# Spreading Layer 2's expert gates over the partitions on TensorE instead of through DRAM

## The chip, the cores and the metric

The kernel runs on one of the eight cores of a Trainium2 chip. The metric is the device time of the whole program in microseconds (us), lower is better; the time given is the median of several runs. The kernel before has a median of 1565.0 us over three runs (1563.73, 1565.0, 1570.41).

## The reference, cut to what matters

The program takes x, of four batches x 512 tokens x 128 features in fp32, through four layers of three residual steps each: an FFN, an attention, an FFN. Every FFN step is x + 0.5 * FFN(LN(x)), every attention step x + attn(LN(x)). The change touches the two FFNs of Layer 2, which weigh eight experts by the two largest of eight logits:

```python
def _L2_ffn_ref(x, w_gate, w_in, w_out):
    xt = x.reshape(-1, D)
    logits = (xt @ w_gate.T).astype(jnp.float32)
    top_logits, top_idx = jax.lax.top_k(logits, TOP_K)
    top_gates = jax.nn.softmax(top_logits, axis=-1).astype(x.dtype)
    gates = (jax.nn.one_hot(top_idx, E, dtype=x.dtype) * top_gates[..., None]).sum(axis=1)
    y = jnp.zeros_like(xt)
    for e in range(E):
        h = xt @ w_in[e].T
        y = y + gates[:, e:e + 1] * (h @ w_out[e].T)
    return y.reshape(B, S, D)
...
x = x + 0.5 * _L1_ffn_ref(_layernorm(x, axis=-1), ...)
x = x + 0.5 * _L2_ffn_ref(_layernorm(x, axis=-1), ...)
x = x + _L2_attn_ref(_layernorm(x, axis=-1), ...)
x = x + 0.5 * _L2_ffn_ref(_layernorm(x, axis=-1), ...)
x = x + 0.5 * _L3_ffn_ref(_layernorm(x, axis=-1), ...)
```

Layer 2's attention is a gated linear recurrence over the tokens. Layer 3's FFN sends each token to two of eight experts with limited capacity. There is no nonlinearity between w_in and w_out in Layer 2, so the kernel multiplies the two beforehand into one 128x128 matrix m_e per expert (`prep_l2`, L1197), and y becomes the sum over e of (gate_e * LN(x)) times m_e.

## The kernel before, in words

**Tiling.** A batch is a tile of 128 partitions (tokens) x 4 token groups x 128 features. The batches go in two pairs, [0, 1] and [2, 3]. Matmuls want the features on the partitions, so a normalized batch is transposed on TensorE into one PSUM bank and copied by ScalarE to a 128x512 tile nT: features on the partitions, tokens along the row (`normed_T`, L1022; `transposed`, L176, L180). PSUM is handed out one bank at a time from a ring of eight (`bank`, L56).

**The chain.** L1475 to L1489 hold the stretch that matters. For each pair, the generator `behind` runs Layer 1's second FFN (`l1_ffn`, L1058), Layer 2's first FFN (`l2_ffn`, L1237), its attention (`l2_attn`, L1290), its second FFN and Layer 3's routing (`Mixture.tokens`, L283). `skewed` (L1404) interleaves the two pairs step by step, the second one eight steps behind the first; a step ends at each `yield`. VectorE, ScalarE, TensorE and SyncE's DMA queue are then put in order by a scheduler with a cost model of its own. GpSimd alone is in manual order: its instructions stay as written. After the chain come Layer 3's experts (`experts`, L405), its attention and the rest.

**One Layer 2 FFN of one pair.** (1) The norms: statistics on VectorE (L153, L154), the root on GpSimd (L157 to L162), the scaling on ScalarE (L167). (2) The eight logits of every token on TensorE (`scored`, L1038), the two largest on VectorE (`route`, L205), their sigmoid weights on ScalarE (L1250, L1252). (3) The gates, one tile of 128 tokens x 8 groups x 8 experts (L1254 to L1257). (4) The gates must weigh nT, whose rows run along the tokens, so every one of nT's 128 partitions needs the gate of each token, for each expert. `to_rows` (L1047) transposes the gates of a batch to 8 experts x 512 tokens (L1051), ScalarE copies them out of PSUM (L1053), and SyncE's queue writes them to DRAM (L1055). From there two DMAs per batch (L1265) read four experts each, repeated for all 128 partitions, 1 MB each, into tiles with the tag "spread" (six buffers). (5) VectorE multiplies each expert's 128x512 gates by nT, in place (L1275). (6) TensorE adds up 8 experts x 4 token groups of 128x128 matmuls in one bank per batch (L1278), and VectorE adds half of it to x (L1287). Steps 4 to 6 read:

```python
            rows = to_rows(pool, gates, x, f"{b}_{tag}")
            for u in range(2):
                half = pool.tile([P, NC, S], FP, name=f"gb{u}{b}_{tag}", tag="spread", bufs=6)
                nc.sync.dma_start(
                    half.rearrange("p e s -> p (e s)"),
                    rows[u * NC : (u + 1) * NC, :].rearrange("e s -> (e s)").partition_broadcast(P),
                )
```

**Around it.** Layer 1's FFN uses `to_rows` too and spreads its gates into tiles cb of the same "spread" buffers (L1083, L1085); its matmuls are L1110, L1111 and L1098. Layer 2's attention has its projections at L1298, two activations at L1300 and L1302, a scan over the tokens at L1307 and its output matmuls at L1311. Layer 3's routing makes logits (L322), ranks (L368, L369), and then scatters each token's row to its experts' places in DRAM by indirect DMAs that GpSimd issues (L395), after copies of counts (L392); for pair [2, 3], batch 2 goes three steps ahead of batch 3. Layer 3's experts begin by fetching what was scattered (L415, L417, L426, L436, L442). The attentions elsewhere in the program use 32-row groups of TensorE for their scores (`product`, L586, L587): four matmuls that contract over 32 partitions each, into four banks.

Of the kernel before, what the change touches and what calls it, by code (L numbers as in the profile page):

```python
# [9 lines left out]
FP = mybir.dt.float32  # L10
I32 = mybir.dt.int32
AF = mybir.ActivationFunctionType
ALU = mybir.AluOpType
# [4 lines left out]
P = 128  # L18
# [23 lines left out]
def kernel(ctx: ExitStack, tc: tile.TileContext, a: dict, out: bass.AP):  # L42
# [1004 lines left out]
    def to_rows(pool, gates, i, tag):  # L1047

        pc = bank(f"gT_{tag}")
        for t in range(NT):  # L1050
            nc.tensor.transpose(pc[:E, t * P : (t + 1) * P], gates[:, i * NT + t, :], ident)  # L1051
        gT = pool.tile([E, S], FP, name=f"gT_{tag}", tag="gT")
        nc.scalar.copy(gT, pc[:E, :])  # L1053
        rows = dram.tile([E, S], FP, name=f"rows_{tag}", tag=f"rows_{tag}")
        nc.sync.dma_start(rows, gT)  # L1055
        return rows

    def l1_ffn(pool, i, bs):  # L1058
        tag = f"f1{i}_{bs[0]}"
        G = len(bs) * NT  # L1060
        nTs = yield from normed_T(pool, bs, tag)
        plg = scored(nTs, l1["gate"], tag)
        sc = pool.tile([P, G, E], FP, name=f"sc_{tag}", tag="sc1")
        nc.scalar.activation(sc, plg, AF.Sigmoid)
        yield
        m1, s1 = route(pool, sc, G, "0")
        rest = without(pool, sc, m1, G, -4.0, "0")
# [12 lines left out]
        for x, b in enumerate(bs):  # L1080
            rows = to_rows(pool, comb, x, f"{b}_{tag}")

            cb = pool.tile([P, NC, S], FP, name=f"cb{b}_{tag}", tag="spread", bufs=6)  # L1083
            for u in range(2):
                nc.sync.dma_start(  # L1085
                    cb[u * I1 : (u + 1) * I1],
                    bass.AP(tensor=rows.tensor, offset=rows.offset + u * S, ap=[[0, I1], [2 * S, NC], [1, S]]),
                )
            cbs.append(cb)
        order = [NC] + list(range(NC))  # L1090
        for x, b in enumerate(bs):
# [13 lines left out]

            for k, c in enumerate(order):
                gw = l1["wg"][:, c * P : (c + 1) * P] if c < NC else l1["sg"]
                uw = l1["wu"][:, c * P : (c + 1) * P] if c < NC else l1["su"]
                ps = pair(f"gu{c}_{b}_{tag}")
                nc.tensor.matmul(ps[0], gw, nTs[x], start=True, stop=True)  # L1110
                nc.tensor.matmul(ps[1], uw, nTs[x], start=True, stop=True)  # L1111
                h = pool.tile([P, S], FP, name=f"h{c}_{b}_{tag}", tag="h1", bufs=6)
                nc.scalar.activation(h, ps[0], AF.Silu)
                nc.vector.tensor_tensor(h, h, ps[1], ALU.mult)
                if c < NC:
                    nc.vector.tensor_tensor(h, h, cbs[x][:, c, :], ALU.mult)
# [120 lines left out]
    def l2_ffn(pool, i, bs):  # L1237
        tag = f"f2{i}_{bs[0]}"
        G = len(bs) * NT
        nTs = yield from normed_T(pool, bs, tag)  # L1240
        lg = scored(nTs, l2["gate"], tag)
        yield
        m1, v1 = route(pool, lg, G, "0")
        rest = without(pool, lg, m1, G, -3.0e38, "0")
        m2, v2 = route(pool, rest, G, "1")

        apart = pool.tile([P, G], FP, name=f"apart_{tag}", tag="apart")
        nc.vector.tensor_tensor(apart, v1, v2, ALU.subtract)
        g1 = pool.tile([P, G], FP, name=f"g1_{tag}", tag="g1")
        nc.scalar.activation(g1, apart, AF.Sigmoid)  # L1250
        g2 = pool.tile([P, G], FP, name=f"g2_{tag}", tag="g2")
        nc.scalar.activation(g2, apart, AF.Sigmoid, scale=-1.0)  # L1252
        yield
        gates = pool.tile([P, G, E], FP, name=f"gates_{tag}", tag="comb")  # L1254
        nc.vector.tensor_tensor(m1, m1, bc(g1, [P, G, E]), ALU.mult)
        nc.vector.tensor_tensor(m2, m2, bc(g2, [P, G, E]), ALU.mult)
        nc.vector.tensor_tensor(gates, m1, m2, ALU.add)  # L1257
        yield

        gb = []  # L1260
        for x, b in enumerate(bs):
            rows = to_rows(pool, gates, x, f"{b}_{tag}")
            for u in range(2):
                half = pool.tile([P, NC, S], FP, name=f"gb{u}{b}_{tag}", tag="spread", bufs=6)
                nc.sync.dma_start(  # L1265
                    half.rearrange("p e s -> p (e s)"),
                    rows[u * NC : (u + 1) * NC, :].rearrange("e s -> (e s)").partition_broadcast(P),
                )
                gb += [half[:, e, :] for e in range(NC)]
        yield  # L1270
        for x, b in enumerate(bs):

            po = bank(f"y{b}_{tag}").rearrange("p (t d) -> p t d", d=D)
            for e in range(E):
                nc.vector.tensor_tensor(gb[x * E + e], gb[x * E + e], nTs[x], ALU.mult)  # L1275
            for e in range(E):
                for t in range(NT):
                    nc.tensor.matmul(  # L1278
                        po[:, t, :],
                        gb[x * E + e][:, t * P : (t + 1) * P],  # L1280
                        l2["m"][:, e, :],
                        start=(e == 0 and t == 0),
                        stop=(e == E - 1 and t == NT - 1),
                    )
                if e % 4 == 3:
                    yield
            nc.vector.scalar_tensor_tensor(xs[b], po, 0.5, xs[b], ALU.mult, ALU.add)  # L1287
            yield

    def l2_attn(pool, bs):  # L1290
# [168 lines left out]
    with tc.tile_pool(name="weights12", bufs=1) as mid:  # L1459
        pools["w"] = mid  # L1460
        prep_l1()
        with tc.tile_pool(name="raw2", bufs=1) as pool:
            made = prep_l2(pool)
            next(made)
            next(made)
            f01.experts(l0["w"], made.send)
            whole(made)
        for b in range(NB):
            whole(f01.combine(b))
        with tc.tile_pool(name="ffn10", bufs=2) as pool:  # L1470
            whole(skewed([l1_ffn(pool, 0, bs) for bs in pairs], 5))

        l1_attn(lambda pool: prep_l3_ffn(xs[0]))

        def behind(pool, bs):  # L1475
            yield from l1_ffn(pool, 1, bs)
            yield from l2_ffn(pool, 0, bs)
            yield from l2_attn(pool, bs)
            yield from l2_ffn(pool, 1, bs)
            if bs[0] == 0:  # L1480
                yield from f30.tokens(bs, l3["gate"], "scalar", pool, later=4)
            else:
                yield from skewed([f30.tokens([b], l3["gate"], "scalar", pool) for b in bs], 3)

        with tc.tile_pool(name="chain", bufs=2) as pool:
            decay = pool.tile([P, S], FP, name="decay", tag="decay", bufs=1)
            nc.gpsimd.memset(decay, 0.9)
            with tc.manual_schedule(engines={mybir.EngineType.Pool}):
                whole(skewed([behind(pool, bs) for bs in pairs], 8))  # L1489
        pools["w"] = wpool  # L1490
# [44 lines left out]
```

## Time and profile before

| | |
|---|---|
| median of three runs | 1565.0 us |
| the profiled execution, its own time | 1562.17 us |
| its span, first to last instruction | 1560.5 us |
| TensorE matmuls (PE) | 1264.9 us busy, 81% |
| TensorE weight loads (PEld) | 821.3 us busy, 53% |
| VectorE (DVE) | 864.1 us busy, 55% |
| ScalarE (ACT) | 712.9 us busy, 46% |
| GpSimd (POOL) | 655.7 us busy, 42% |
| DMA traffic | 123.12 MB |
| mean granted TensorE clock | 0.893 of full |

The profile is of one execution, which the hardware recorded; its lines are sorted by source line and engine. A line such as "L1278 PE MATMUL y_f<-m,gb_f 128*128 128x128 f32" names source line, engine, operation, output and inputs, tile of the array and shape. An fp32 matmul leaves two records, so a count of 8 is four matmuls. In a timeline, the first column is the start in us from the beginning of the span and the second how long the row's instructions took together; the text in square brackets is how long the engine sat idle before and what ended that. SPq is SyncE's DMA queue. The chain from Layer 1's second FFN to Layer 3's routing lies between about 777 and 1051 us of the span. The four Layer 2 FFNs have their gates done at 845.7 (pair 0, first), 879.5 (pair 1, first), 936.9 (pair 0, second) and 975.4 us (pair 1, second). The tags of these four in the order named are f20_0, f20_2, f21_0 and f21_2.

### The profile page before, as it was taken

What the parts mean: (1) busy time and instruction counts of PE and PEld (TensorE: products, weight loads), DVE (VectorE), ACT (ScalarE), POOL (GpSimd) and SP (SyncE); (2) the same over time, 40 slices, a digit from 0 to 9 for tenths busy, and PEclk for the clock granted to TensorE, in tenths of its full rate; (3) what the DMA queues carried; (4) which work ended last, traced back from release to release, by engine and by line L of the source; (5) the groups of instructions that cost most, each with busy time, mean ns of one, the idle gap of its engine ahead of it and who ended that gap; (6) DMA issues with size and microseconds to landing.
All of it is one profiled execution on the core that took longest, in us unless ns stands there. A gap on an engine that the chain in (4) does not pass through costs nothing. (4 is left out here: it accounts for less than half of the span.)

```text
span 1560.5 us, 28691 instructions
## 1 busy us (share of the span) xinstructions
PE 1264.9 (81%) x10523; PEld 821.3 (53%) x10523; DVE 864.1 (55%) x2947; ACT 712.9 (46%) x1487; POOL 655.7 (42%) x789
## 2 busy tenths in 40 slices
PE   4777998995969688989988676718779999998394
PEld 3455676773756455766756655616533343333273
DVE  5335676773325365766556455515367787774343
ACT  1234876871443165768643322203325655564041
POOL 3455767872520176777501111273632214212253
PEclk9997999996979888999999778758979999999597
DMA  7420240002515474442033302214204000000223
GB/s 231 129 57 8 77 164 12 9 13 64 148 35 109 126 226 123 136 123 69 2 78 116 135 0 109 114 50 114 64 21 171 14 3 13 12 5 15 75 79 105
DMA packets 103092, 123.12 MB, mean 79 GB/s; under 512 B 9404, under 2 KB 74152, under 8 KB 100904
## 3 DMA queue, kind: packets, MB, share of 16 engines
q1 hardware_dynamic: 96296, 108.07, 23.2%
q0 software_dynamic: 6656, 13.22, 2.6%
q8 instruction: 84, 1.38, 0.4%
q14 instruction: 56, 0.46, 0.1%
HBM read 79.27 MB, written 41.98 MB: 78 GB/s over the span
## 5 line engine op out<-in xcount | busy, mean ns | idle before, releaser
L605 POOL TENSOR_SCALAR sc_a<-sc_a,top_a 128x128 f32<-128x128 f32 (+3 forms) x256 | 275.4, 1091 | 112.1 <-DVE top_a L604 72.2
L587 PE MATMUL s_a<-k_a,q_a 32*128 32x512 f32 (+3 forms) x1536 | 267.1, 549 | 17.9 <-DMA k_a<-fac_a 14.2
L692 ACT ACTIVATE w_a<-t_a 128x512 f32<-128x512 f32 x256 | 140.4, 595 | 119.7 <-PE t_a L587 94.8
L628 PE MATMUL t_a<-ident,sc_a 128*128 128x128 f32 x1280 | 172.3, 282 | 6.0 <-DVE top_a L608 5.6
L489 POOL DMA_INDIRECT res_f<-y_f,back_f x112 | 109.7, 980 | 141.8 <-ACT y_f L488 101.3
L587 PE MATMUL t_a<-ql_a,k_a 32*128 32x512 f32 x512 | 168.8, 643 | 0.5 <-DVE low_a__12599 L672 0.2
L628 PEld LDWEIGHTS t_a<-ident,sc_a 128*128 128x128 f32 x1280 | 145.1, 144 | 36.8 <-issue 13.8
L617 ACT ACTIVATE sc_a<-sc_a,top_a 128x128 f32<-128x128 f32 (+3 forms) x256 | 135.0, 577 | 23.8 <-DVE top_a L608 23.6
L587 PEld LDWEIGHTS s_a<-k_a,q_a 32*128 32x128 f32 x1536 | 93.7, 188 | 88.9 <-issue 43.1
L637 ACT ACTIVATE w_a<-t_a 128x256 f32<-128x256 f32 (+2 forms) x192 | 94.2, 526 | 64.2 <-PE t_a L628 63.7
L395 POOL DMA_INDIRECT disp_f<-n_f,to_f x96 | 94.3, 983 | 66.8 <-issue 58.8
L501 PE MATMUL o_f<-w_l,h_f 128*128 128x128 f32 (+1 forms) x896 | 113.0, 279 | 3.8 <-DVE o_f L483 3.3
L501 PEld LDWEIGHTS o_f<-w_l,h_f 128*128 128x128 f32 (+1 forms) x896 | 103.0, 184 | 14.7 <-DVE o_f L483 6.0
L466 PE MATMUL h_f<-dT_f,w_l 128*128 128x320 f32 (+1 forms) x256 | 107.8, 559 | 2.8 <-ACT dT_f L444 2.8
L157 POOL TENSOR_SCALAR rs_f<-mv_f 128x4 f32<-128x4 f32 (+1 forms) x23 | 6.5, 281 | 233.4 <-DVE mv_f L154 232.7
L650 PE MATMUL acc_a<-w_a,vpad 128*32 128x128 f32 x2560 | 98.4, 280 | 0.6 <-DVE top_a L604 0.6
L639 ACT COPY w_a<-t_a 128x256 f32<-128x256 f32 (+2 forms) x192 | 93.7, 528 | 6.7 <-PE t_a L628 6.5
L672 DVE TENSOR_REDUCE low_a__12599<-s_a 128x1 f32<-128x512 f32 x128 | 82.1, 685 | 26.3 <-PE t_a L587 18.5
L608 DVE CUSTOM_DVE_ANT_0 sc_a<-s_a,future 128x128 f32<-128x128 f32 (+3 forms) x128 | 62.3, 487 | 57.2 <-PE s_a L587 44.2
L672 DVE TENSOR_REDUCE low_a__12597<-s_a 128x1 f32<-128x512 f32 x128 | 81.3, 683 | 20.5 <-PE t_a L587 15.1
L608 DVE CUSTOM_DVE_ANT_0 sc_a<-s_a,table 128x128 f32<-128x128 f32 (+3 forms) x128 | 62.4, 487 | 53.0 <-PE s_a L587 52.5
L488 ACT ACTIVATE y_f<-o_f,d_f 128x128 f32<-128x128 f32 (+1 forms) x112 | 38.8, 394 | 105.9 <-DVE o_f L483 102.3
(337 smaller groups left out, 2260.8 us busy)
## 6 DMA issues: line engine op xcount, KB each, us to landing
gb_f<-rows_f SPq DMA_DIRECT2D x16, 1024.0 KB
fac_a<-fac_a_sb SPq DMA_DIRECT2D x36, 256.0 KB
disp_f<-zeros_f SPq DMA_DIRECT2D x4, 2080.0 KB
d_f<-disp_f SPq DMA_DIRECT2D x32, 260.0 KB
w_l<-in_L_ffn_w_dram SPq DMA_DIRECT2D x16, 512.0 KB
cb_f<-rows_f SPq DMA_DIRECT2D x16, 512.0 KB
q_a<-fac_a SPq DMA_DIRECT2D x32, 256.0 KB
k_a<-fac_a SPq DMA_DIRECT2D x32, 256.0 KB
```

Source lines behind the costliest of these rows:

```text
L395: nc.gpsimd.indirect_dma_start(out=self.to[c][i0 + t][:, :], out_offset=bass.IndirectOffsetOnAxis(ap=to[:, c, t : t + 1], axis=0), in_=ns[ ...
L466: nc.tensor.matmul(ps[u][:, :cap], w1[:, e, (c + u) * P : (c + u + 1) * P], dT, start=True, stop=True)
L489: nc.gpsimd.indirect_dma_start(out=self.back[e * per + s][:, :], out_offset=bass.IndirectOffsetOnAxis(ap=back[:m, s : s + 1], axis=0), in_ ...
L501: nc.tensor.matmul(po[:m, s, :], h[:, c, s * P : s * P + m], w2[:, e, c, :], start=(c == 0), stop=(c == NC - 1),)
L587: nc.tensor.matmul(ps[:, n0:n1], q[r : r + SLOT, i * P : (i + 1) * P], k[r : r + SLOT, n0:n1], start=True, stop=True)
L605: nc.gpsimd.tensor_scalar(sc, sc, top, None, ALU.subtract)
L608: nc.vector.tensor_tensor_reduce(sc, banks[r][:, :n], more, -1.0, HUGE, ALU.add, ALU.min, top)
L617: nc.scalar.activation(sc, sc, AF.Exp, bias=top, scale=-1.0)
L628: nc.tensor.transpose(ps[:, x * n + j * P : x * n + (j + 1) * P], st["sc", u, i, r0 + x][:, j * P : (j + 1) * P], ident,)
L650: nc.tensor.matmul(st["acc", u][r * SLOT : (r + 1) * SLOT, i * P : (i + 1) * P], vpads[b % 2][:, j, g * 4 + r, :], st["w", u, i, r][:, j * ...
L672: nc.vector.tensor_reduce(st["low", u][:, i, c : c + 1], ps, AX.X, ALU.max, negate=True)
L692: nc.scalar.activation(w, ps, AF.Exp)
```

## The change

The gates no longer go through DRAM. They are written into a tile of 128 tokens x 8 groups x 128 columns that lives as long as the chain, one per pair, set to zero once on GpSimd. Expert e = 2r + u has column 32r + u, so the transpose of a group, now 128x128, puts it on partition 32r + u: each of the four 32-row groups r of TensorE holds two experts. One ScalarE copy of 128x512 per batch brings this into SBUF (gT). Two constant tiles `row[u]` of 128x128 hold ones on the partitions p with p % 32 = u, zeros elsewhere. Four matmuls that contract over 32 partitions, one in each row group, of `row[u]` and gT then put the gates of four experts on all 128 partitions, each in a PSUM bank of its own; VectorE multiplies each bank by nT into a tile of the new tag "gb" (eight buffers). A batch takes two such rounds, u = 0 and 1. The sixteen y matmuls of a round are issued one round later (`down`), after the next round's four.

The DMAs of Layer 2's rows and broadcasts disappear; Layer 1's FFN keeps its own, and "spread" has four buffers in place of six. An FFN of Layer 2 has one `yield` less. Line numbers after: zeroed tiles L1506, `row` L1511 to L1514, gates L1261, transposes L1267, copy L1269, y matmuls L1281, residual L1290, row-group matmuls L1298, multiplies L1301.

```diff
@@ l1_ffn
-            cb = pool.tile([P, NC, S], FP, name=f"cb{b}_{tag}", tag="spread", bufs=6)
+            cb = pool.tile([P, NC, S], FP, name=f"cb{b}_{tag}", tag="spread", bufs=4)
@@ l2_ffn
-        gates = pool.tile([P, G, E], FP, name=f"gates_{tag}", tag="comb")
+
+        gates = l2["gates", bs[0]]
+        parted = gates.rearrange("p g (r c) -> p g r c", c=SLOT)[:, :, :, : E // 4]
         nc.vector.tensor_tensor(m1, m1, bc(g1, [P, G, E]), ALU.mult)
         nc.vector.tensor_tensor(m2, m2, bc(g2, [P, G, E]), ALU.mult)
-        nc.vector.tensor_tensor(gates, m1, m2, ALU.add)
+        for u in range(E // 4):
+            one, two = (m.rearrange("p g (r u) -> p g r u", r=4)[:, :, :, u] for m in (m1, m2))
+            nc.vector.tensor_tensor(parted[:, :, :, u], one, two, ALU.add)
         yield
-
-        gb = []
+        gTs = []
         for x, b in enumerate(bs):
-            rows = to_rows(pool, gates, x, f"{b}_{tag}")
-            for u in range(2):
-                half = pool.tile([P, NC, S], FP, name=f"gb{u}{b}_{tag}", tag="spread", bufs=6)
-                nc.sync.dma_start(
-                    half.rearrange("p e s -> p (e s)"),
-                    rows[u * NC : (u + 1) * NC, :].rearrange("e s -> (e s)").partition_broadcast(P),
-                )
-                gb += [half[:, e, :] for e in range(NC)]
+            pc = bank(f"gT{b}_{tag}")
+            for t in range(NT):
+                nc.tensor.transpose(pc[:, t * P : (t + 1) * P], gates[:, x * NT + t, :], ident)
+            gT = pool.tile([P, S], FP, name=f"gT{b}_{tag}", tag="gT2", bufs=2)
+            nc.scalar.copy(gT, pc)
+            gTs.append(gT)
         yield
...
+        def down(x, u):
+
+            if u == 0:
+                pos[x] = bank(f"y{bs[x]}_{tag}").rearrange("p (t d) -> p t d", d=D)
+            for r in range(4):
                 for t in range(NT):
                     nc.tensor.matmul(
-                        po[:, t, :],
-                        gb[x * E + e][:, t * P : (t + 1) * P],
-                        l2["m"][:, e, :],
...
+                        pos[x][:, t, :],
+                        gb[x, u, r][:, t * P : (t + 1) * P],
+                        l2["m"][:, r * (E // 4) + u, :],
...
+        rounds = [(x, u) for x in range(len(bs)) for u in range(E // 4)]
+        for x, u in rounds + [(None, None)]:
+            if x is not None:
+                banks = [bank(f"gate{u}{r}_{x}_{tag}") for r in range(4)]
+                for r in range(4):
+                    rows = slice(r * SLOT, (r + 1) * SLOT)
+                    nc.tensor.matmul(banks[r], l2["row"][u][rows, :], gTs[x][rows, :], start=True, stop=True)
+                for r in range(4):
+                    gb[x, u, r] = pool.tile([P, S], FP, name=f"gb{u}{r}_{x}_{tag}", tag="gb", bufs=8)
+                    nc.vector.tensor_tensor(gb[x, u, r], banks[r], nTs[x], ALU.mult)
+            if (x, u) != rounds[0]:
+                down(*rounds[rounds.index((x, u)) - 1 if x is not None else -1])
             yield
@@ the chain's setup
+            for bs in pairs:
+                l2["gates", bs[0]] = pool.tile([P, 2 * NT, P], FP, name=f"gates{bs[0]}", tag=f"gates{bs[0]}", bufs=1)
+                nc.gpsimd.memset(l2["gates", bs[0]], 0.0)
+
+            l2["row"] = []
+            for u in range(E // 4):
+                flag = pool.tile([P, 1], FP, name=f"flag{u}", tag=f"flag{u}", bufs=1)
+                nc.vector.tensor_reduce(flag, ident.rearrange("p (r c) -> p r c", c=SLOT)[:, :, u], AX.X, ALU.add)
+                row = pool.tile([P, P], FP, name=f"row{u}", tag=f"row{u}", bufs=1)
+                nc.vector.tensor_copy(row, flag.to_broadcast([P, P]))
+                l2["row"].append(row)
```

More of the change, by code (lines that the diff above doesn't have):

```diff
@@ L1270, in l2_ffn @@
-        yield
[L1271 to L1276, printed above, removed]
+            pc = bank(f"gT{b}_{tag}")
+            for t in range(NT):
+                nc.tensor.transpose(pc[:, t * P : (t + 1) * P], gates[:, x * NT + t, :], ident)
+            gT = pool.tile([P, S], FP, name=f"gT{b}_{tag}", tag="gT2", bufs=2)
@@ L1277, in l2_ffn @@
+            nc.scalar.copy(gT, pc)
+            gTs.append(gT)
+        yield
+        pos, gb = {}, {}
+        def down(x, u):
+            if u == 0:
+                pos[x] = bank(f"y{bs[x]}_{tag}").rearrange("p (t d) -> p t d", d=D)
+            for r in range(4):
                 for t in range(NT):
                     nc.tensor.matmul(
-                        po[:, t, :],
-                        gb[x * E + e][:, t * P : (t + 1) * P],
-                        l2["m"][:, e, :],
-                        start=(e == 0 and t == 0),
@@ L1283, in l2_ffn @@
-                        stop=(e == E - 1 and t == NT - 1),
-                    )
-                if e % 4 == 3:
-                    yield
-            nc.vector.scalar_tensor_tensor(xs[b], po, 0.5, xs[b], ALU.mult, ALU.add)
+                        pos[x][:, t, :],
+                        gb[x, u, r][:, t * P : (t + 1) * P],
+                        l2["m"][:, r * (E // 4) + u, :],
+                        start=(u == 0 and r == 0 and t == 0),
+                        stop=(u == E // 4 - 1 and r == 3 and t == NT - 1),
+                    )
@@ new lines, in down @@
+            if u == E // 4 - 1:
+                b = bs[x]
+                nc.vector.scalar_tensor_tensor(xs[b], pos[x], 0.5, xs[b], ALU.mult, ALU.add)
+        rounds = [(x, u) for x in range(len(bs)) for u in range(E // 4)]
[10 more added lines that the diff above has]
+                down(*rounds[rounds.index((x, u)) - 1 if x is not None else -1])
```

## The prediction

> **What bounds the kernel now.** I read the page's busy shares first: TensorE (PE) is busy 81% of the span, VectorE (DVE) 55%, so PE decides on average. The change is confined to the chain of Layer 1's last FFN, Layer 2 and Layer 3's routing, so I went on to the list of waits for 835 to 1060 us, where this chain lies. Its columns are total us, number of waits, and the longest.
>
> ```profile
> DVE n_f L415 <- DMA disp_f<-n_f,to_f: 27.9, 1, 27.9
> ...
> DVE gb_f L1275 <- DMA gb_f<-rows_f: 21.6, 4, 8.3
> PE y_f L1278 <- DVE gb_f L1275: 20.7, 4, 7.1
> ...
> PE T_f L180 <- ACT n_f L167: 3.0, 1, 3.0
> ```
>
> There are four Layer 2 FFN instances (two FFNs, two pairs of batches), and each waits once: DVE for the broadcast gates, PE for DVE. So 20.7 us of PE idle time stand in front of exactly the step that the change replaces. Next I read the timeline of the last instance, to see the wait's parts.
>
> ```profile
> 975.13 0.23 DVE L1257 TENSOR_TENSOR gates_f<-mask,mask 128x64 f32<-128x64 f32 x1
> 975.41 1.87 PE L1051 MATMUL gT_f<-ident,gates_f 128*8 128x128 f32 x8 [6.26 <-DVE gates_f L1257]
> ...
> 977.01 1.03 ACT L1053 COPY gT_f<-gT_f 8x512 f32<-8x512 f32 x2
> 977.60 0.76 SPq L1055 DMA_DIRECT2D rows_f<-gT_f  x2
> ...
> 979.12 1.82 SPq L1265 DMA_DIRECT2D gb_f<-rows_f  x4
> ...
> 983.65 2.50 DVE L1275 TENSOR_TENSOR gb_f<-gb_f,nT_f 128x512 f32<-128x512 f32 x4 [8.29 <-DMA gb_f<-rows_f]
> ...
> 984.44 1.83 PE L1278 MATMUL y_f<-m,gb_f 128*128 128x128 f32 x7 [5.46 <-DVE gb_f L1275]
> ```
>
> From gates to first multiply are 8.3 us (975.36 to 983.65), of which 6 lie between the write of the rows (977.60) and the landing of the first broadcast. The other three legs take 8.3, 8.3 and 8.7 us. The stretches beside it show a second loss; the number after the busy times is the granted PE clock.
>
> ```profile
> 982.00:984.00 2.00, 0.00 (x0) 0.00 (x0) 0.35 (x1) 0.00 (x0) 0.00 (x0) 0.69 1.00 410
> 984.00:986.00 2.00, 1.56 (x7) 1.59 (x8) 2.00 (x4) 0.00 (x0) 0.00 (x0) 0.50 1.01 422
> 986.00:988.00 2.00, 2.00 (x12) 2.00 (x11) 2.00 (x5) 0.00 (x0) 0.00 (x0) 0.50 1.01 426
> ...
> 990.00:992.00 2.00, 2.00 (x21) 2.00 (x20) 0.00 (x0) 0.00 (x0) 0.00 (x0) 1.00 0.10 41
> ```
>
> After the idle time PE runs at half clock for some 5 us. The same 16 matmuls (32 records) of L1278 take 3.74 us at full clock (at 896.51) but 6.41, 6.48 and about 6.25 us right after the second, third and fourth wait: 2.5 to 2.7 us lost three times. The first wait is short (2.7 us) and the clock stays up.
>
> Does a gain in this chain reach the end? The chain that ended last names almost only PE work after 1125 us, so I followed what hangs on the chain's last result, x of batch 3 (L1287, 1005.06 us):
>
> ```profile
> 1007.35 0.22 POOL L157 TENSOR_SCALAR rs_f<-mv_f 128x4 f32<-128x4 f32 x1 [3.61 <-DVE mv_f L154]
> ...
> 1009.94 1.13 POOL L395 DMA_INDIRECT disp_f<-n_f,to_f  x1 [0.15 <-POOL n_f L392]
> ```
>
> GpSimd (POOL) keeps the written order; it waits for DVE's statistics of batch 3 at 1007.35, then issues 32 scatters at 1.265 us each, and the 27.9-us wait at L415 above ends only after the last, at 1052.68. PE's 34.5-us wait for the fetched rows (L442) follows. So an earlier x of batch 3 moves the scatters and all behind them one for one.
>
> **What the Trainium skill says.** "TensorE: Matmul & The Clock Gate", Part 3 (packing small matmuls): four K=32, N=512 tiles in four row groups give 3.07 times the rate. The trace has this form in the attention's scores:
>
> ```profile
> 750.91 1.14 PE L587 MATMUL s_a<-k_a,q_a 32*128 32x512 f32 x8
> 751.99 0.33 PE L628 MATMUL t_a<-ident,sc_a 128*128 128x128 f32 x1
> ```
>
> Eight records are four matmuls: 1.08 us until the next instruction starts, against 4 x 0.86 = 3.44 for ordinary 128x512 matmuls (two of L1298 take 1.71): a factor of 3.2, in agreement. In 500 to 800 us, 16 such groups are 19.7 us busy, 1.23 each. "TensorEngine Tiling (Array Packing)", Key Properties and Gotcha 1: changing the tiling mode drains TensorE, and each row tile needs its own PSUM bank. The 1.08 us stand between instructions of other modes, so a drain is in them; the banks are a risk below. "TensorE: Matmul & The Clock Gate", Part 1: idle time of about 3.4 us halves the clock and as much work restores it. The trace agrees roughly: idle from 979.0, halved at about 983.6; full again after some 5 us of work. "DMA: Bandwidth & Descriptors", Anatomy of one DMA, gives about 2 us fixed per DMA, mostly completion; its fit is for GpSimd's queue. Two chained DMAs on SP measured 6 us here, so the order of size agrees.
>
> **The change part by part.**
> *Removed.* Eight row writes and sixteen 1-MB broadcasts: 24 issues on SP and 16 MB. SP has nothing due behind them in the chain, and no one else waits for the DMA rings there, so this is worth only its wait. The new leg: one more DVE add (0.2), four transposes (half of 1.87), one ACT copy (0.6, the 128x512 form takes 0.59), the first group (1.1, or 2.2 at half clock), one multiply (0.7): about 3.5 to 4.6 us until the first y matmul, against 9.1 now (975.36 to 984.44). In that time PE has the eight transposes, the second group, and the other pair's work. I leave 0.7 us of idle time for each of legs two to four (copy and multiply, less one group), none for the first, where Layer 1's matmuls cover most of the wait already. With the shorter gap I expect the clock to be up when y begins.
> *Added on PE.* Four groups per instance, 16 in all. Price 1.08 us, ends 1.23 (busy) and, overlap failing, 3.44. None are hidden: PE is the leading engine in y. 4 x 1.08 = 4.3 per instance. The transposes are 128 instead of 8 columns wide; those of L180, of that form, take the same 1.04 us for eight at full clock: no cost.
> *Changed on DVE.* The 64 multiplies read PSUM in place of SBUF: 0.687 us (L1114) against 0.685. Four are 2.7 us per round, PE needs 3.74 + 1.08 = 4.8: hidden under PE, at no cost while PE is the slower one.
> *ACT.* Copies of 128x512 in place of 8x512: 0.59 against 0.57; nothing.
> *Setup.* Two memsets on POOL (about 0.9 us each, half of the 1.8 of 128x2048) between the memset of 0.9 and the first norm, and four small DVE operations. POOL then waited 1.35 us for DVE at 779.21, so some 0.5 us stay; but Layer 1's first normalized tile is ready at 785 and its transposes start only at 797.18: hidden. Without that cover it would cost 0.5.
> *Moved.* By the instruction orders, outside the Layer 2 FFNs nothing changes places. At the third leg, the transposes that today wait 3.0 us instead of 1.04 for ACT (960.86) come to stand inside y: 2.0 us regained. DVE has Layer 3's routing of batch 2 between the last instance's multiplies; a routing step that waits would hold them.
>
> Sum, leg by leg (idle gone + clock + moved, against groups and idle left): first −2.7 + 4.3 = +1.6. Second −5.4 − 2.6 + 4.3 + 0.7 = −3.0. Third −7.1 − 2.7 − 2.0 + 4.3 + 0.7 = −6.8. Fourth −5.5 − 2.5 + 4.3 + 0.7 = −3.0. Together −11.2. A group takes four of eight banks at once, and its last bank comes free only by a multiply of the group before it or by the other pair's ACT and DVE work; the trace shows no such wait, so its bounds are 0 and about 1.1 us per instance (a group's slot lost); I take 0.5, in all +2.0. Below zero is excluded, since no bank is freed sooner. That gives −9.2. The profiled execution took 1562.2 us (span 1560.5 and 1.7 around it): 1553.0. The runs' median is 1565.0, 2.8 above: 1555.8, say 1556.
>
> **The rivals.** *B, the wait is replaced.* The clock stays halved at the start of y (the three 2.5s are not regained, +7.8) since the new steps are short with gaps: −9.2 + 7.8 = −1.4, 1564. For it: in the fourth leg PE does transposes from 975.4 to 979 and still starts y at half clock. Against: 980 to 983 showed full clock, it fell during the wait. *C, slower: the groups do not overlap.* 16 groups at p us cost 16p against 17.3 in my sum: −9.2 − 17.3 + 16p. It decides from p = 1.66 upward. In pairs (p about 2.2) it is +8.7, 1574; one after the other (3.44) +28.5, 1594. Against it: the same form runs at 1.08 and 1.23. For it: this group's four outputs must find four banks free at once, which could space them out. *D, nothing reaches the end*: the scatter train starts when it does now, because something else than batch 3's x holds POOL: 1565. Against it: POOL waited 3.61 us just there.
>
> **How the numbers follow.** As forecast (A) 0.64, 1554 to 1561 (no bank waits: −11.2, 1554; 1.1 each: −6.8, 1558; 1.23 a group: +2.4 more); B 0.22; D 0.06; C 0.08. I count 0.5% (7.8 us) as what a measurement of this kernel can tell from no change: faster means under 1557.2. Of A, 0.52 lies there and 0.12 above; with B and D, no change has 0.40; C is slower, 0.08. The range from 1550 (no bank waits, none of the 2.1 us of idle time left, and the first leg's 1.6 covered: −14.9) to 1566 holds A, B and D and leaves out C and a little of the rest.
>
> **What would show it.** L1275's and L1278's waits for DMA and DVE gone, under 3 us left in front of y; 16 groups of eight 32x512 records at 1.1 to 1.2 us each; y's first 32 records at 3.7, not 6.4 us; the step to x of batch 3 and the first scatter both 9 us earlier (1000.8 from 1009.9), and L415's wait ending as much earlier. Wrong, if y starts at half clock, if DVE idles inside y for routing steps, if groups last over 1.66 us, or if later stages lengthen by what the chain gives.

## The result, and the profile after

The changed kernel takes 1558.1 us in the median of six runs (1553.6 to 1560.3), against 1566.5 us for six runs of the kernel before: a ratio of 0.9945, with a 95% interval of 0.9933 to 0.9957, or 8.4 us less. The forecast was 1556 against 1565, 9 less. The profiled execution took 1557.3 us, with a span of 1555.6 (before: 1562.2 and 1560.5).

The list of waits for the same stretch, 835 to 1060 us, of the changed kernel:

```profile
DVE n_f L415 <- DMA disp_f<-n_f,to_f: 28.1, 1, 28.1
...
DVE x L1290 <- PE y_f L1281: 17.8, 7, 4.9
...
DVE gb_f L1301 <- PE gate_f L1298: 2.8, 4, 1.2
```

The waits for the broadcast (21.6 us on DVE, 20.7 on PE) are gone, and a line of PE waiting for the multiplies no longer appears. DVE waits for PE instead, at the end of y: PE leads, as forecast. The wait behind the scatters is as long as before (28.1 against 27.9): nothing there was shortened, it was moved.

The fourth leg on the timeline (start, duration):

```profile
972.06 0.32 DVE L1261 TENSOR_TENSOR gates<-mask,mask 128x32 f32<-128x32 f32 x2
...
975.20 1.08 ACT L1269 COPY gT_f<-gT_f 128x512 f32<-128x512 f32 x2
...
976.41 2.00 PE L1298 MATMUL gate_f<-gT_f,row 32*128 32x512 f32 x16
...
977.57 1.29 DVE L1301 TENSOR_TENSOR gb_f<-gate_f,nT_f 128x512 f32<-128x512 f32 x2 [0.57 <-PE gate_f L1298]
...
978.34 0.94 PE L1281 MATMUL y_f<-m,gb_f 128*128 128x128 f32 x6
```

From the gates to the first y matmul are still 6.0 us (972.38 to 978.34), not the forecast's 3.5 to 4.6: ScalarE copies the gates only after Layer 3's two normalized tiles. But PE sits idle in none of it. It does transposes, Layer 3's logits and two of the four groups (a group: the four row-group matmuls of one round), and the clock is up when y begins. The stretches show it (PE's busy time first, the granted clock after the five busy times):

```profile
974.00:976.00 2.00, 2.00 (x18) 2.00 (x18) 0.00 (x0) 1.28 (x3) 0.00 (x0) 0.90 0.00 0
976.00:978.00 2.00, 2.00 (x21) 1.29 (x20) 0.88 (x3) 1.82 (x3) 0.00 (x0) 1.00 0.04 8
978.00:980.00 2.00, 2.00 (x18) 1.66 (x15) 2.00 (x6) 0.00 (x0) 0.00 (x0) 1.00 0.00 0
```

y's first 16 matmuls (32 records) take 3.84 us here. In the second and the third leg they take as long; before, they took 6.25 to 6.48 us in these three legs:

```profile
892.69 3.84 PE L1281 MATMUL y_f<-m,gb_f 128*128 128x128 f32 x32
...
946.12 3.84 PE L1281 MATMUL y_f<-m,gb_f 128*128 128x128 f32 x32
```

The groups' price, by form, in 840 to 1010 us (busy us, mean ns of one record, idle before):

```profile
L1281 PE MATMUL y_f<-m,gb_f 128*128 128x128 f32 x512 | 60.7, 277 | 0.0
...
L1298 PE MATMUL gate_f<-gT_f,row 32*128 32x512 f32 x128 | 18.9, 634 | 0.4 <-ACT gT_f L1269 0.4
```

Sixteen groups are 18.9 us busy, 1.18 each; from the start of a group until the next instruction starts are 1.07 (852.18 to 853.25). y has no idle time before it and is 60.7 us busy in place of 67.5. GpSimd's first step for batch 3 and the first scatter:

```profile
1001.05 0.22 POOL L157 TENSOR_SCALAR rs_f<-mv_f 128x4 f32<-128x4 f32 x1 [3.52 <-DVE mv_f L154]
...
1003.65 1.13 POOL L395 DMA_INDIRECT disp_f<-n_f,to_f  x1 [0.15 <-POOL n_f L392]
```

Before, they stood at 1007.35 and 1009.94. The chain itself must be read from its own start, because the time ahead of it differs from one execution to the next. The next table, from the timelines, gives the us from the start of GpSimd's memset of 0.9 to the arrival of each leg's logits (DVE's first maximum) and to the first scatter.

| kernel | leg 1 | leg 2 | leg 3 | leg 4 | first scatter |
|---|---|---|---|---|---|
| before | 62.4 | 94.6 | 152.3 | 191.9 | 232.6 |
| after | 62.4 | 96.7 | 152.4 | 186.5 | 224.3 |
| first FFN alone | 64.0 | 98.2 | 152.8 | 191.9 | 232.6 |
| second FFN alone | 62.4 | 94.7 | 152.5 | 186.6 | 224.5 |
| broadcasts unread | 62.5 | 96.7 | 152.5 | 186.7 | 224.6 |
| groups twice | 62.4 | 100.1 | 159.0 | 195.7 | 237.2 |
| ordinary matmuls | 62.6 | 105.5 | 170.4 | 211.9 | 261.2 |
| before, clock kept (4 each) | 62.6 | 94.9 | 149.8 | 188.9 | 230.2 |
| before, clock kept (5, 7, 6) | 62.4 | 94.5 | 149.5 | 188.2 | 227.6 |
| after, clock kept | 62.4 | 96.7 | 152.4 | 186.6 | 223.7 |
| hybrid | 62.5 | 94.6 | 146.3 | 175.0 | 220.4 |
| hybrid, clock kept | 62.4 | 94.5 | 146.3 | 175.0 | 214.0 |

The chain is 8.3 us shorter. The pair of profiled spans differs by 4.9 only, since the chain began 2.0 us later (779.33 against 777.34) and 1.4 more lay behind the first scatter (551.95 against 550.56). Both vary as much between other traces (starts from 775.5 to 783.2; in the kernel before with the clock kept by four matmuls 550.3 behind the scatter, with each group twice 553.0), so neither is put down to the change, and the six runs a side agree with the chain.

Each row of the table is one execution, and TensorE's clock can shift it. Up to the first leg's logits TensorE has the same order of work in all twelve kernels, and yet they come 1.6 us later in the kernel with the first FFN alone. Differences of 1 to 2 us between rows need the runs, or a cause on the timeline, beside them.

### The profile page after: what moved, and what is told of

Read it like the earlier page. It is cut to its first block, busy times and chain, and to the rows that moved or that the text cites. A ratio compares the mean times of both kernels' runs of the same rounds, so it can differ in the third digit from the quotient of the medians.

```text
span 1555.6 us, 28883 instructions
## 1 busy us (share of the span) xinstructions
PE 1279.9 (82%) x10651; PEld 823.0 (53%) x10651; DVE 866.6 (56%) x2955; ACT 713.2 (46%) x1487; POOL 657.2 (42%) x791
## 5 line engine op out<-in xcount | busy, mean ns | idle before, releaser
L587 PE MATMUL s_a<-k_a,q_a 32*128 32x512 f32 (+3 forms) x1536 | 266.5, 548 | 17.1 <-POOL k_a L1183 13.8
L692 ACT ACTIVATE w_a<-t_a 128x512 f32<-128x512 f32 x256 | 140.4, 595 | 119.6 <-PE t_a L587 94.9
L395 POOL DMA_INDIRECT disp_f<-n_f,to_f x96 | 94.6, 985 | 66.7 <-issue 58.8
L608 DVE CUSTOM_DVE_ANT_0 sc_a<-s_a,table 128x128 f32<-128x128 f32 (+3 forms) x128 | 62.4, 488 | 52.9 <-PE s_a L587 52.4
```

The costliest lines, as they stand in the source:

```text
L395: nc.gpsimd.indirect_dma_start(out=self.to[c][i0 + t][:, :], out_offset=bass.IndirectOffsetOnAxis(ap=to[:, c, t : t + 1], axis=0), in_=ns[ ...
L587: nc.tensor.matmul(ps[:, n0:n1], q[r : r + SLOT, i * P : (i + 1) * P], k[r : r + SLOT, n0:n1], start=True, stop=True)
L608: nc.vector.tensor_tensor_reduce(sc, banks[r][:, :n], more, -1.0, HUGE, ALU.add, ALU.min, top)
L692: nc.scalar.activation(w, ps, AF.Exp)
```

## The experiments

Four of the kernels below (second FFN alone, broadcasts unread, clock kept with 5, 7, 6, and clock kept in the changed kernel) ran on a chip on which the kernel before took 1585.6 us, so the ratios are what is compared, not the times.

**Each group twice.** The four row-group matmuls of a round are issued twice:

```diff
                 for r in range(4):
                     rows = slice(r * SLOT, (r + 1) * SLOT)
                     nc.tensor.matmul(banks[r], l2["row"][u][rows, :], gTs[x][rows, :], start=True, stop=True)
+                for r in range(4):
+                    rows = slice(r * SLOT, (r + 1) * SLOT)
+                    nc.tensor.matmul(banks[r], l2["row"][u][rows, :], gTs[x][rows, :], start=True, stop=True)
```

> Every row-group matmul of the gates is issued twice into the same bank, the second one overwriting the first with the same values: sixteen groups more. Theory (PE leads in y and in the legs, the chain's end moves the program's end one for one): 16 x 1.07 = 17.1 us more than the changed kernel, less some 1.5 us where PE waits anyway in the third leg, so +15 to +17, which is +7 to +9 against the kernel before. Rival (PE has slack in these stretches or the scatters start when they do anyway): under +5 against the changed kernel, still faster than before.

Measured: 1568.7 us, ratio to before 1.0015 (1.0007 to 1.0023); in the chain 12.9 us more than the changed kernel. The direction is the theory's, the size is less. The timeline says why:

```profile
848.34 1.14 PE L1298 MATMUL gate_f<-gT_f,row 32*128 32x512 f32 x8
849.30 1.04 PE L1301 MATMUL gate_f<-gT_f,row 32*128 32x512 f32 x8
850.27 0.38 PE L1098 MATMUL o_f<-wd1T,h_f 128*128 128x128 f32 x1
```

Two groups take 1.93 us from first start to the next instruction, one takes 1.07: the second adds 0.86. That is the time of one ordinary 128x512 matmul. The other 0.21 us are spent once for each time that PE goes over to row groups and back. 16 x 0.86 = 13.8; the missing 0.9 fits the idle time of the third leg, 1.5 us in the changed kernel and 0.6 here. PE has hardly any slack in the chain. By the two ratios the program takes 11.0 us more than the changed kernel, which within their intervals is what the chain lost; against the kernel before it is 2.3 us (1.1 to 3.6), of 4.6 in the chain.

**Ordinary matmuls in place of row groups.** The case of rival C of the prediction, built. The rows of `row` are not built:

```diff
-                    rows = slice(r * SLOT, (r + 1) * SLOT)
-                    nc.tensor.matmul(banks[r], l2["row"][u][rows, :], gTs[x][rows, :], start=True, stop=True)
+                    nc.tensor.matmul(banks[r], ident[:, r * SLOT + u : r * SLOT + u + 1].to_broadcast([P, P]), gTs[x], start=True, stop=True)
```

> The gates are spread by ordinary matmuls over all 128 rows, one 128x512 per expert, with a column of the identity as weights, instead of four 32-row matmuls at once. Theory (the row groups overlap; that is what makes the change pay): 16 x (3.44 - 1.07) = +38 us against the changed kernel, less 1 to 3 for drains and idle time that go: +35 to +38, slower than before by 26 to 30. Rival (the groups are no faster than ordinary matmuls, or PE has slack): under +10 against the changed kernel.

Measured: 1590.3 us, ratio 1.0161 (1.0145 to 1.0176), slower than before; the chain is 36.9 us longer than in the changed kernel (in the slowest of the five executions, 1595.8 us). On the timeline a round's four now take 3.44 us:

```profile
852.31 3.60 PE L1297 MATMUL gate_f<-gT_f,ident 128*128 128x512 f32 x8
855.75 1.95 PE L1098 MATMUL o_f<-wd1T,h_f 128*128 128x128 f32 x16
```

So the change pays only because a group's four matmuls run at once: without that, the same way around DRAM loses 25 us.

This kernel also shows what going over to row groups costs the work beside a group. The 16 y matmuls between two rounds, first in the changed kernel, then here:

```profile
861.14 3.84 PE L1281 MATMUL y_f<-m,gb_f 128*128 128x128 f32 x32
```

```profile
860.97 3.73 PE L1281 MATMUL y_f<-m,gb_f 128*128 128x128 f32 x32
```

From their start to that of the next round are 3.77 us between groups (to 864.91) and 3.57 here (to 864.54). Of the 0.2 more about half falls behind a group and half ahead of the next, since in the changed kernel the y that follows a group but does not precede one takes 3.67 (865.98 to 869.65). So a group that stands alone costs about 1.27 us and not 1.07; 0.4 of it are for the change of tiling.

**The broadcasts kept, unread.**

```diff
             gTs.append(gT)
+            rows = dram.tile([E, S], FP, name=f"rows_{b}_{tag}", tag=f"rows_{b}_{tag}")
+            nc.sync.dma_start(rows, gT[:E, :])
+            for u in range(2):
+                half = pool.tile([P, NC, S], FP, name=f"gone{u}{b}_{tag}", tag="spread", bufs=4)
+                nc.sync.dma_start(
+                    half.rearrange("p e s -> p (e s)"),
+                    rows[u * NC : (u + 1) * NC, :].rearrange("e s -> (e s)").partition_broadcast(P),
+                )
```

> The changed kernel, with the eight row writes and the sixteen 1-MB broadcasts still issued after ScalarE's copies, into spread tiles that nobody reads. Theory (only the wait for them cost time, not the issues on SyncE's queue nor the 16 MB): within 1.5 us of the changed kernel. Rival (part of the gain came from the traffic that is gone, or from SyncE's shorter list): 3 us or more slower than the changed kernel.

Measured: ratio 0.9934 (0.9917 to 0.9951), and the table's line is the changed kernel's to 0.3 us. The 24 issues and 16 MB have no cost of their own that was measured; what the change removed was the wait, with what the wait did to the clock.

**The kernel before, with TensorE kept at work in the wait.**

```diff
                 gb += [half[:, e, :] for e in range(NC)]
+        if (i, bs[0]) != (0, 0):
+            idle = bank(f"idle_{tag}")
+            for r in range(4):
+                nc.tensor.matmul(idle, ident, nTs[-1], start=True, stop=True)
         yield
```

> The kernel before, with four 128x512 matmuls into an unread bank after the transposes of the gates of the second, third and fourth leg, so that PE works while the broadcast is under way; nothing else is changed and the wait stays. Theory (2.5 to 2.7 us of each of these three waits' cost is the halved clock after it): 5 to 8 us faster than before, y's first 32 records in 3.7 to 4.5 us instead of 6.4. Rival (the halved clock only follows the wait and would cost nothing, or the filler delays what it stands before): within 1 us of before, or slower.

Measured: 1562.9 us, ratio 0.9987 (0.9979 to 0.9996), 2.4 us less in the chain: less than half of the 5 to 8 that were expected. Four matmuls filled only the second leg's wait. In the third, 3.6 us of idle time were left and the first 32 records of y still took 6.42 us, in the fourth 2.1 and 5.44. So the number was raised to 5, 7 and 6:

```diff
-            for r in range(4):
+            for r in range({(0, 2): 5, (1, 0): 7, (1, 2): 6}[i, bs[0]]):
```

> The kernel before with matmuls into an unread bank in the second, third and fourth wait, as in clock4, but five, seven and six of them in place of four each, since in clock4 idle time of 3.6 and 2.1 us was left in the third and fourth wait and y still ran at half clock there (6.42 and 5.44 us for the first 32 records, 3.81 in the second leg). Theory: with the idle time under 1.5 us the clock is up in all three, 6 to 8 us faster than before. Rival (the clock is no cost by itself): no faster than clock4, 2.7 us under before.

Measured: ratio 0.9954 (0.9936 to 0.9971), 7.3 us (4.6 to 10.1), and 5.0 us less in the chain. y after the second, third (two lines) and fourth wait:

```profile
894.68 3.81 PE L1282 MATMUL y_f<-m,gb_f 128*128 128x128 f32 x32 [1.03 <-DVE gb_f L1279]
...
949.53 3.84 PE L1282 MATMUL y_f<-m,gb_f 128*128 128x128 f32 x32 [1.45 <-DVE gb_f L1279]
...
964.28 5.37 PE L1282 MATMUL y_f<-m,gb_f 128*128 128x128 f32 x32
...
986.69 3.81 PE L1282 MATMUL y_f<-m,gb_f 128*128 128x128 f32 x32
```

All three now start at full clock, with the wait for the broadcast still there (22.3 us on VectorE): 5 us or somewhat more of the wait's cost was the clock alone. In the third leg part was lost again: behind a later wait for ScalarE's tiles, which stood there before too, the next 32 records now take 5.37 us in place of 3.74.

**One FFN alone.** The changed `l2_ffn` for the second FFN and the former one for the first, and then the other way round ("spread" has four buffers in both). The former one stands beside it as `l2_ffn_dram`; of the edit only the call is given, in short:

```diff
-            yield from l2_ffn(pool, 0, bs)
+            yield from l2_ffn_dram(pool, 0, bs)
```

> Only Layer 2's second FFN (legs three and four) takes the row groups; its first FFN (legs one and two) goes through DRAM as before. Theory (legs add up as their steps were sized): the first two legs together gained 1.4 us in the changed kernel's profile against before (+1.9 and -3.3), legs three and four 8.3, so this kernel lies about 8 us under before, within 2 us of the changed kernel. Rival (the order that the scheduler chooses for the whole chain decides more than the legs): off from that by over 3 us, with the other order to be seen on TensorE.

> Only Layer 2's first FFN (legs one and two) takes the row groups, the second one goes through DRAM as before: the other half of the kernel named second. The forecast's steps gave +1.6 and -3.0 for these two legs, -1.4 in all. Theory after the runs so far (in the changed kernel the logits of the third leg come at the same distance from the chain's begin as before, 152.4 against 152.3 us, since the 3.3 us won in the second leg go to steps at half clock before the third, and the second FFN alone had the whole gain): within 1 us of before. Rival (each FFN brings half of the gain): about 4 us faster than before.

Measured: the second FFN alone 0.9937 (0.9920 to 0.9955), the first alone 0.9991 (0.9978 to 1.0005). Legs three and four alone bring the whole gain. What the first FFN's change brings can't be told from zero, nor from the forecast's 1.4 us: the interval goes from 3.4 us less to 0.8 more. Its row in the table has a shift that isn't the edit's. Layer 1's matmuls just ahead of the first leg's logits ran in part at half clock here, in the changed kernel in 1.02 us each:

```profile
839.41 1.91 PE L1110 MATMUL gu_f<-nT_f,sg1T 128*128 128x512 f32 x2
841.12 1.50 PE L1111 MATMUL gu_f<-nT_f,su1T 128*128 128x512 f32 x2
```

From the first leg's logits to the third's this kernel is 1.1 us shorter than before (88.8 against 89.9), the changed kernel is not (90.0).

**Only the first leg through DRAM.** The call, again in short:

```diff
-            yield from l2_ffn(pool, 0, bs)
+            yield from (l2_ffn_dram if bs[0] == 0 else l2_ffn)(pool, 0, bs)
```

> The changed kernel, but the first leg (first FFN of batches 0 and 1) takes the way through DRAM as before; the other three use the row groups. The spread tiles have four buffers. Theory (legs add up, and in the first leg Layer 1's matmuls cover most of the broadcast, so the four groups cost 1.6 to 1.9 us there): 1.5 to 2 us faster than the changed kernel, about 10 faster than before. Rival (legs don't add up, or the broadcast into fewer buffers starts later): the same as the changed kernel or up to 3 us slower.

Measured: 1552.5 us, ratio 0.9915 (0.9902 to 0.9928), better than both kernels, by more than the 1.5 to 2 us under the changed kernel that were expected (4.7 by the ratios, 3.9 in the chain). The first leg gives its 2.1 us. The rest is more than the sum of the legs: by the logits of leg four the hybrid is 11.5 us ahead of the changed kernel, and then loses 7.6 of it. The scheduler put TensorE in another order. In the hybrid, the second leg's gates are transposed before the attention's tiles and not among them, and ScalarE copies them 103.8 us after the chain's start in place of 108.5. That this order explains the whole difference is read from the two timelines; it was not tried by itself.

**The hybrid, with TensorE kept at work in the fourth leg.** What the hybrid loses in its last leg is on its timeline:

```profile
963.21 2.01 PE L180 MATMUL T_f<-ident,n_f 128*128 128x128 f32 x5 [4.18 <-ACT n_f L167]
965.15 2.07 PE L1298 MATMUL gate_f<-gT_f,row 32*128 32x512 f32 x2
967.15 0.90 PE L180 MATMUL T_f<-ident,n_f 128*128 128x128 f32 x3
967.98 2.08 PE L1298 MATMUL gate_f<-gT_f,row 32*128 32x512 f32 x6
970.00 3.58 PE L322 MATMUL lg_f<-gate,nT_f 128*128 128x8 f32 x16
973.51 2.09 PE L1298 MATMUL gate_f<-gT_f,row 32*128 32x512 f32 x8
975.53 4.98 PE L1281 MATMUL y_f<-m,gb_f 128*128 128x128 f32 x32
```

After 4.2 us of idle time everything runs at half clock for some 15 us, until 978 us in the midst of y, and transposes stand in the middle of a group and part it in two. The edit:

```diff
             gTs.append(gT)
+        if (i, bs[0]) == (1, 2):
+            idle = bank(f"idle_{tag}")
+            for r in range(4):
+                nc.tensor.matmul(idle, ident, gTs[-1], start=True, stop=True)
         yield
```

> The hybrid kernel with four 128x512 matmuls into an unread bank after the transposes of the gates of the fourth leg, where its TensorE sits idle for 4.2 us and then runs at half clock for 17 us (four groups or parts of them at 2.1 us, logits 3.6 us, the first 32 records of y 5.0 us); the order of everything else on TensorE is the same. Theory (these steps are PE's own work on the way to x of batch 3, so the halved clock costs there): 3 to 5 us faster than the hybrid kernel, a ratio to before of about 0.989. Rival (as in the kernel named warm, what follows the gap is paced by ScalarE's normalized tiles): within 1 us of the hybrid kernel, 0.9915.

Measured: 1548.0 us, ratio 0.9879 (0.9858 to 0.9899), 18 us below before and the fastest of all. The same stretch:

```profile
962.03 3.70 PE L1274 MATMUL idle_f<-gT_f,ident 128*128 128x512 f32 x8 [0.78 <-ACT gT_f L1269]
965.57 2.89 PE L180 MATMUL T_f<-ident,n_f 128*128 128x128 f32 x8
968.39 1.14 PE L1302 MATMUL gate_f<-gT_f,row 32*128 32x512 f32 x8
969.46 1.95 PE L322 MATMUL lg_f<-gate,nT_f 128*128 128x8 f32 x16
971.34 1.14 PE L1302 MATMUL gate_f<-gT_f,row 32*128 32x512 f32 x8
972.41 3.84 PE L1285 MATMUL y_f<-m,gb_f 128*128 128x128 f32 x32
```

The chain is 6.4 us shorter than the hybrid's, more than the 3 to 5 expected. The order did not stay the same, against the expectation: the transposes now stand ahead of the first group, and it is no longer parted. How much of the 6.4 is that and how much the clock was not taken apart; the logits' 1.95 us in place of 3.58 and y's 3.84 in place of 4.98 are clock, 2.8 us.

**The changed kernel, with TensorE kept at work.** The same means in the changed kernel's own gaps:

```diff
         lg = scored(nTs, l2["gate"], tag)
+        if bs[0] == 2:
+            warm = bank(f"warm_{tag}")
+            for r in range(4):
+                nc.tensor.matmul(warm, ident, nTs[-1], start=True, stop=True)
@@ l2_attn
         b_in = l2["b_in"]
+        if bs[0] == 2:
+            warm = bank(f"warm_{tag}")
+            for r in range(5):
+                nc.tensor.matmul(warm, ident, decay, start=True, stop=True)
```

> The changed kernel, with matmuls into an unread bank where its TensorE still sits idle for 4.7 to 5.1 us and then runs at half clock: four 128x512 after the logits of the second and of the fourth leg, five after the last output matmul of the attention of batches 0 and 1. The order of everything else on TensorE is the same. Theory (idle time on TensorE costs twice, as itself and by the halved clock after it, wherever PE's steps are on the way): 3 to 8 us faster than the changed kernel. Rival (what follows these gaps waits for VectorE and ScalarE, so PE's clock does not count there, or the matmuls hold up what they stand before): within 1.5 us, or slower.

Measured: ratio 0.9937 (0.9920 to 0.9954), 0.6 us less in the chain than in the changed kernel: the rival's case. The transposes after the gap wait for ScalarE one by one (1.68 us in the second leg), and in the attention the clock was down again when the projections came (3.78 us for four records, as without the filler). Here keeping PE at work paid where PE's own steps followed, and not where another engine paced it.

## Why the prediction was right, step by step

The sum held: 9.2 forecast, 8.3 in the chain and 8.4 in the medians. Not all of its terms did.

- *The idle time in front of y goes* (20.7 us): right. Broadcasts that are still made and not waited for cost nothing that was measured.
- *A group costs 1.08 us*: right as far as it was counted (1.07), and a group's four matmuls do overlap. The 0.2 us beside it were left out. With 14 changes of tiling (two pairs of groups stand together) the 16 groups come to about 19.5 us, an estimate from 16 x 0.86 and 14 x 0.41; the sum had 17.3. The rival's case, built as a kernel of ordinary matmuls, costs what it was priced at (+28.5 forecast against before, +28.6 in the chain, +25 in the time).
- *The clock is up when y begins* (7.8 us in three legs): right in kind, since y's first 32 records take 3.84 us in all four legs. Alone, without the rest of the change, it was worth 5.0 us in the chain; the runs' 4.6 to 10.1 leave the size open. Rival B is out. The reading behind it was loose: the prediction has the clock halved at about 983.6, but its own line of 982 to 984 us (0.69) puts the fall near 982.8: PE had then been idle for 3.8 us and not for 4.6.
- *Bank waits, +2.0*: mostly wrong. In the first leg the rounds follow each other at 4.84 us (860.07, 864.91), a group and 16 matmuls with no gap. Of the groups at full clock only the very last takes longer, 1.52 us until y starts at 989.31, 0.45 more than 1.07: a weight load of it waits for a multiply of the round before (L1301), which stood behind batch 2's routing steps on VectorE.

```profile
987.79 1.60 PE L1298 MATMUL gate_f<-gT_f,row 32*128 32x512 f32 x8
```

- *First leg, +1.6*: 2.1 measured. *Second leg, −3.0*: it is −3.3 up to GpSimd's root for the attention, 135.9 us after the start against 137.1. But then 1.2 us are given back before the third leg, which leaves −2.1, and the first FFN as a whole brings nothing in this pair of traces. The forecast had what the second leg wins reach the end; here it did not. The logits of the third leg ran at half clock throughout, in the kernel before they had it back midway. First the changed kernel, then the kernel before:

```profile
928.23 3.42 PE L1038 MATMUL lg_f<-gate2T,nT_f 128*128 128x8 f32 x16
```

```profile
927.40 2.20 PE L1038 MATMUL lg_f<-gate2T,nT_f 128*128 128x8 f32 x16
```

In the kernel with the first FFN alone these logits take 1.85 us, and there the gain does reach the third leg. So this loss is the clock's, and whether it comes does not follow from the change alone.
- *Third leg, −6.8*: 5.4. More idle time is left than the 0.7 us allowed: the second batch's output matmuls stand ahead of the second group on PE and wait 1.16 us for the scan, and the first group waits 0.38 us for the copy. The 0.2 us beside each of the four groups are enough for the rest. *Fourth leg, −3.0*: 2.9.
- *Moves the end one for one*: right for what was gained. The scatters begin 8.3 us earlier after the chain's start, and L415 8.1. In the other direction somewhat less arrived: 2.3 of 4.6 us with each group twice, 25 of 28.6 with ordinary matmuls. Where the rest went was not followed.
- *Setup hidden*: right; TensorE does not wait for the normalized tile in either kernel. That the first leg's logits come at 62.4 us in both is luck in part: on the way the changed kernel is 1.7 us behind through the clock (the transposes of that tile come 21.5 us after the memset, against 19.8) and makes it up.

So the near hit of the total is in part luck. The four legs measured, +2.1, −2.1, −5.4 and −2.9 us, fall 2.9 us short of their own forecast of −11.2, and the 2.0 us that were set aside for bank waits, of which 0.45 came, made up for most of it.

## What to carry to other kernels

Price a wait on TensorE with the clock that it costs afterwards, and look at the work right behind it: if it is TensorE's own, a few matmuls into an unread bank can keep the clock up, here at no cost that was seen; where another engine paced it, they brought 0.6 us at most. A detour by DMA that other work covers, as in the first leg here, should stay: a replacement on the leading engine is then only an added cost. And where a scheduler sets the order, measure a change leg by leg from a fixed point: the same edit was worth 5.4 us in one leg and cost 2.1 in another, and leaving it out of one leg moved the whole order. A single trace is not enough for 1 or 2 us, since the clock alone moved the first leg by 1.6.

## What the runs showed of the hardware

A group of four fp32 matmuls with 32 rows each takes as long as one ordinary 128x512 matmul, 0.86 us. Going over to the other tiling and back costs about 0.4 us: 0.21 until the next instruction starts (1.07 against 0.86), and 0.2 on the matmuls beside the group (3.77 against 3.57 for 16 of them). One of the eight adds that write the changed kernel's gates took 1293 ns where the median is 210; it stood beside GpSimd's add of a 128x512 tile:

```profile
L1261 DVE TENSOR_TENSOR gates<-mask,mask x8: 197/210/1293, 847.6 to 972.2; 128x32 f32<-128x32 f32 x8
```

```profile
L960 POOL TENSOR_TENSOR x<-x,bout x2: 1265/1266/1268, 883.5 to 885.0; 128x512 f32<-128x512 f32 x2
```

The first line is of DVE over the chain, the second of GpSimd in 877 to 888 us (shortest, median and longest in ns). The add ended at 884.80, when GpSimd's instruction of 883.46 was over; in the hybrid, whose add came at 881.4, all adds lie between 203 and 218 ns. In the five other kernels that have this leg's add in the changed kernel's place it took 1286 to 1291 ns. "SBUF — State Buffer" of the Trainium skill, in its section on the two separate sides, says that DVE with two SBUF inputs and GpSimd, when it reads SBUF, share an exclusive port pair, and that the later one blocks until the other's instruction is over; the 1.29 us against 1.27 agree.

The chain's times are often very steady: the changed kernel and its two variants that leave the order as it is come to the legs at the same times to 0.2 us, on two chips. They are not always: the kernel with the first FFN alone, with the same order up to there, comes to the first leg 1.6 us later, through matmuls at half clock. Where the clock comes back within such a chain, as in the logits above, so differs even between executions of the same order, and why it returned in one kernel there and not in the other stays open.
